# Patch layer of a four-layer stack: half of some B products made on ScalarE from turned operands, partitions ordered state by channel, other C products on GpSimd, and a new plan of slots

## The chip, the cores and the metric

The kernel runs on one core of a Trainium2 chip. A core has five engines with a queue of instructions each: PE (TensorE: matrix products and transposes), DVE (VectorE), ACT (ScalarE: functions from tables, and copies), POOL (GpSimd) and SP (SyncE, which here issues DMAs). Sixteen DMA engines move data between HBM and the on-chip memory SBUF; PE writes into a second on-chip memory, PSUM. The metric is the device time of one execution in microseconds, and the median of 15 runs is given.

## The reference

The input x is (8, 96, 64, 64) in float32. Four layers are added to it in turn, each of the form x = x + layer(gn(x)), where gn is a group normalization: a selective scan over single channels (L0), a gate in the frequency domain (L1), the patch layer (L2) and a deformable 3x3 convolution (L3). Only L2 differs between the two kernels. Cut to what matters:

```python
xz = einsum('bchw,ec->behw', x, in_proj_w)          # 96 -> 2 x 192 channels
xin, z = split(xz, 2); z = silu(z)
t = gelu(batchnorm(conv3x3(xin)))                   # 192 channels
offset = tanh(conv1x1(t)) * 1/(H-1)                 # two offsets for each pixel
x_s = grid_sample_bilinear(xin, grid + offset)
xt = x_s in patches of 4 x 4 pixels                 # L = 16 steps each
xs4 = [xt, xt turned (w,h), and both reversed]      # 4 directions
dts, Bs, Cs = split(einsum(xs4, x_proj_weight))     # 6, 16 and 16 rows
delta = softplus(einsum(dts, dt_projs_weight) + bias)
# for each direction, channel d (192), state n (16), along the 16 steps:
h = h * exp(delta * A[d, n]) + delta * u * B[n]     # "B product" delta*u*B
y[d] = sum_n h * C[n]                               # "C product" h*C
y = sum of the 4 directions + D * u
out = out_proj(layernorm(y) * z)
```

## The kernel before

**Tiling.** L2 is cut into chunks of 512 pixels (8 rows of 64), 8 chunks for each of the 8 images, 64 in all. In a chunk the 512 pixels are 32 patches of 16 steps, and one scan instruction runs over all of them, since delta is set to a huge number at one end of each patch, so that exp gives 0 and the state starts anew (`edges`, L1546). Per chunk and direction there are 192 channels × 16 states = 3,072 rows of 512 steps. They go in groups of 128 partitions × 2 × 512: 32 channels (`GC2`) by 4 state quads (`HS2`) on the partitions, p = d·4 + s, and two of the four states of a quad in the free dimension; `part` 0 and 1 are the two halves of a quad. That makes 12 groups for one direction and 48 for a chunk (`PER` = 48).

**Slots.** `WideSlots.slot` (L442 to L492) issues, slot by slot, what each group needs. In slot t:

- on SP, `dd` for slot t+6 (`AHEAD2`): one DMA that copies delta and delta·u of 32 channels to the 128 partitions, each row four times (L458); both parts share it, so it is issued in every other slot;
- on ACT, for slot t+1, two exps of 128x512 with a scale per partition, from dd into a PSUM tile `ps_d` (L466), of which there are three;
- on DVE, the scan of slot t (L1584, 128x1024), from `ps_d` and `dbu` into `ps_d`;
- on PE, the totals for slot t−2: two groups of matrix products with `k_red2` that sum over the states and add up in `ps_y` (L373);
- on POOL, the B product of slot t+2, delta·u from dd times B from `brep`, into `dbu` in SBUF (L485; 8 buffers);
- on DVE, the C product of slot t−1, `ps_d` times `crep` into `dbu` (L490). For a group named in `LATE2` the scan would write to `dbu` and POOL would make that product; `LATE2` is empty.

DVE's order is thus scan(t), C(t−1), scan(t+1), and so on, and the exp of slot t+1 needs the `ps_d` tile that C(t−2) has read.

`brep` and `crep` are the 16 rows of B or C of one direction, spread over 128 partitions as 4 states × 512 (1 MB, two buffers each). `spread` in `direction` (L1568) issues them on SP; the source is 16 rows in HBM (`bcd`). With the four directions numbered n = 0 to 3, B goes out 2 slots ahead of its pair for odd n and 8 ahead for even n, C one slot behind it or 5 ahead.

**The plan.** Everything else of a chunk is placed by hand in the same slots: `sl.at(slot, engine, function)`, counted from the chunk's first slot B or its pair's first slot T, and run on that engine in the order of `slot`. A chunk's two pairs of directions (`ORDER` = 0, 2, 1, 3) have 24 slots each, and each is slots 0 to 5 first half of the channels of the one direction, 6 to 11 the same half and 12 to 17 the second half of the other, 18 to 23 the second half of the first. `front` (the convolution L1280, gelu L1312, offset L1321, tanh L1341, place L1348, bilinear sampling on POOL L1383, a turned copy of xs L1396, inner L1403, both L1425) runs up to 81 slots ahead of a chunk; `pair` makes delta (products L1483, softplus on ACT and POOL, L1495 to L1538); `gates` makes silu(z); `end` normalizes, gates (L1682), projects, adds x (L1686) and stores (L1719).

ACT holds one table of functions at a time. The default in the loop is the one with exp and ln (`LOG_EXP`); gelu, tanh and silu each load their own and load `LOG_EXP` again (L1313, L1342).

Of the kernel before, what the change touches and what calls it, by code (L numbers as in the profile page):

```python
# [57 lines left out]
def shape_constants():  # L58
# [19 lines left out]
    for d in range(GC2):  # L78
        red[d * HS2 : (d + 1) * HS2, 64 + d] = 1.0
# [33 lines left out]
def lay_out(i):  # L113
# [16 lines left out]
    for k in range(4):  # L130
# [28 lines left out]
        .transpose(2, 3, 0, 1, 4)  # L159
# [84 lines left out]
LOG_EXP = "natural_log_exp_and_others"  # L244
FAR = 1e25
AHEAD = 4
AHEAD2, SPREAD2 = 6, 4
LATE2 = ()
# [193 lines left out]
class WideSlots(Slots):  # L442


    def run(self):
        ts = list(self.plan) + [t + d for t in self.groups for d in (-self.ahead, 3)]
        with self.S.tc.manual_schedule():
            for t in range(min(ts), max(ts) + 1):
                self.slot(t)

    def slot(self, t):
        nc, G = self.S.nc, self.groups.get
        g = G(t + self.ahead)
        if g and g.part:
            g.dd = G(t + self.ahead - 1).dd
        elif g:
            g.dd = new(self.pool, [128, 2, NW], "dd", bufs=self.spread)
            nc.sync.dma_start(  # L458
                g.dd.rearrange("p x l -> p (x l)"),
                g.steps().unsqueeze(1).to_broadcast([self.gc, 128 // self.gc, 2 * NW]),  # L460
            )
        g = G(t + 1)
        if g:
            g.da = new(self.psd, [128, 2, NW], "ps_d")
            for i in range(2):
                nc.scalar.activation(  # L466
                    g.da[:, i, :], g.dd[:, 0, :], AF.Exp, scale=g.a[:, i : i + 1]
                )
        self.side(t, "first")
        g = G(t)  # L470
        if g:
            g.h = g.dbu if g.late else g.da
            g.scan(*(v.rearrange("p i l -> p (i l)") for v in (g.h, g.da, g.dbu)))
# [4 lines left out]
        g = G(t - 3)  # L478
# [4 lines left out]
        if g:  # L483
            g.dbu = new(self.pool, [128, 2, NW], "dbu", bufs=8)
            nc.gpsimd.tensor_tensor(  # L485
                g.dbu, g.dd[:, 1:2, :].to_broadcast([128, 2, NW]), g.b(), ALU.mult
            )
        g = G(t - 1)
        if g:
            (nc.gpsimd if g.late else nc.vector).tensor_tensor(g.dbu, g.h, g.c(), ALU.mult)  # L490
        for engine in ("pool", "dve", "sp", "end"):
# [698 lines left out]
def layer2(S, src, dst, st_in, st_out, images, cp, W, ready, finish):  # L1190
# [3 lines left out]
    with ExitStack() as ctx:  # L1194
# [32 lines left out]
        for k in range(4):  # L1227
# [3 lines left out]
        for k in range(2):  # L1231
            t = new(cp, [CH + 1, 2, NW], f"xs{k}")
# [11 lines left out]
        def front(ch, b, pad, xs, c, B):  # L1244
# [4 lines left out]
            def load():  # L1249
                ch["x"] = new(fp, [CH, 10 * IW], "xl")  # L1250
# [50 lines left out]
            for m, slots, last in (  # L1301
                (0, ((-81, 1), (-80, 2), (-79, 1), (-78, 1), (-77, 1), (-76, 1), (-75, 2)), -74),
                (1, ((-67, 1), (-66, 2), (-65, 1), (-64, 1), (-63, 1), (-62, 1), (-61, 2)), -60),
# [7 lines left out]
            def gelu():  # L1311
                nc.scalar.activation(ch["t"], ch["t"], AF.Gelu)  # L1312
                nc.scalar.preload_act_table_set(LOG_EXP)  # L1313

            sl.at(B - 60, "act", gelu)

            def offset(a):
# [16 lines left out]
                sl.at(B - 59 + a, "pe", pe)  # L1334
                sl.at(B - 58 + a, "first", act)
# [4 lines left out]
            def tanh():  # L1340
                nc.scalar.activation(ch["f"], ch["f"], AF.Tanh)  # L1341
                nc.scalar.preload_act_table_set(LOG_EXP)  # L1342

            def place():
# [3 lines left out]
                nc.scalar.activation(f, f, AF.Identity, bias=sl.half[:CH], scale=0.5)  # L1348

            sl.at(B - 57, "act", tanh)  # L1350
            sl.at(B - 56, "act", place)
# [29 lines left out]
            def sampled():  # L1381
                for k in range(2):
                    nc.gpsimd.tensor_tensor(  # L1383
                        xs[:CH, 0, k * 256 : (k + 1) * 256].rearrange("p (n h w) -> p n h w", h=4, w=4),
# [11 lines left out]
            sl.at(B - 44, "act", lambda: nc.scalar.copy(xs[:CH, 1, :], turned(xs[:CH, 0, :])))  # L1396

            def inner(j):


                def pe():
# [4 lines left out]
                        xs[:CH, 0, :],  # L1406
# [9 lines left out]
                sl.at(B - 23 + j, "pe", pe)  # L1416
                sl.at(B - 22 + j, "first", act)
# [4 lines left out]
            def both():  # L1422
                ch["pa"] = new(psa, [128, NW], "ps_a")
                for o in range(2):
                    nc.tensor.matmul(  # L1425
                        ch["pa"], bc_w[:, o].rearrange("c m s -> c (m s)"), xs[:CH, o, :],
                        start=o == 0, stop=o == 1,
                    )

            def both_out():  # L1430
                ch["bc"] = new(fp, [128, NW], "bc")
# [6 lines left out]
            sl.at(B - 20, "pe", both)  # L1438
            sl.at(B - 19, "first", both_out)
            sl.at(B - 19, "sp", both_store)  # L1440

        def gates(ch, pad, T):
            x = pad[:, 1:9, 1 : IW + 1]

            def gate(m):
# [16 lines left out]
                sl.at(T + m, "pe", pe)  # L1462
                sl.at(T + 1 + m, "first", act)
# [8 lines left out]
            sl.at(T + 2, "act", silu)  # L1472

        def pair(ch, xs, n, T):
# [4 lines left out]
            def first(j):  # L1479
                def pe():  # L1480
# [5 lines left out]
                        xs[:, n, :],  # L1486
# [4 lines left out]
                def act():  # L1491
                    if j == 0:
                        st["e"] = new(fp, [128, BLK, NW], "sp_e")
                        st["m"] = new(fp, [128, BLK, NW], "sp_m")
                    nc.scalar.activation(st["e"][:, j, :], st["p"], AF.Abs)  # L1495
                    nc.scalar.activation(st["m"][:, j, :], st["p"], AF.Relu)  # L1496

                sl.at(T - 26 + j, "pe", pe)
                sl.at(T - 25 + j, "first", act)
# [15 lines left out]
            for m, run in enumerate((exp, one, ln, less)):  # L1515
                sl.at(T - 22 + m, "act", run)

            def block(j):
                e, m, w, s = (lambda k=k: st[k][:, j, :] for k in "emws")

                def add():
                    nc.gpsimd.tensor_tensor(m(), m(), s(), ALU.add)  # L1522
# [4 lines left out]
                def delta():  # L1527
                    if j == 0:
                        pr["d"] = new(fp, [128, BLK, 2, NW], "delta", bufs=2)
                    nc.gpsimd.tensor_tensor(pr["d"][:, j, 0, :], m(), w(), ALU.subtract)  # L1530
# [17 lines left out]
                for i, run in enumerate((add, lost, delta, delta_u)):  # L1548
                    t = BLK * i + j
                    t = T - 18 + t + (t > 4)  # L1550
                    sl.at(t, "pool", run)
                sl.at(t + 1, "act", edges)

            for j in range(BLK):
                first(j)
                block(j)
            return pr

        def direction(ch, pr, xs, k, n, T):
# [4 lines left out]
            def spread(name, what, t):  # L1564
                def run():
# [6 lines left out]
                        .unsqueeze(0)  # L1572
                        .to_broadcast([GC2, HS2, 4 * NW]),
# [665 lines left out]
```

## Time and profile before

| | |
|---|---|
| median of 15 runs | 18,137.27 us (18,088.57 to 18,169.72) |
| profiled execution | 18,137.31 us |
| its span | 18,135.5 us |
| 0 to 3873 us | L0, L1, and the start of L2 |
| 3873 to 14,311 us | L2's 64 chunks |
| 14,311 to 18,135.5 us | end of L2, and L3 |
| busy in the span | DVE 89%, POOL 82%, PE 75%, ACT 55%, PE's weight loads 27% |
| DMA | 2,437 MB in 802,718 packets |

How to read the profile. A group of instructions is one line: source line, engine, operation, output and inputs, number; then busy time in us, the mean of one in ns, and the idle time of the engine ahead of them with what ended most of it. Instructions of an engine overlap a little in the records, so that the mean of one is more than the distance from start to start. The timeline has one line for each instruction: start, length, engine, line, operation. Stretches of time are tabulated by windows: length, busy time of each engine, granted clock (1.00 is full speed), share of the 16 DMA engines that were busy, and what they moved.

### The profile page before, as it was taken

Reading aid. Unit: us, or ns where it says so; the run is one execution under the profiler, and the core shown is the slowest. Engines: PE = TensorE matmul, PEld = TensorE weight load, DVE = VectorE, ACT = ScalarE, POOL = GpSimd, SP = SyncE. Lnnn points to the kernel's source line nnn. Section 1 sums busy time; section 2 is a strip of 40 time slices with the busy share of each in tenths; the row PEclk is TensorE's granted clock in tenths of the full one; section 3 lists DMA queues with packets and bytes.
Section 4 is the critical chain, followed back from the end, with each engine's and each line's share of the span. In section 5 each row is a group of like instructions: output and inputs, shape, how many; then the busy total and the mean of one; then the engine's idle time right before and its main releaser. Section 6 shows DMA issues by size and latency. Waiting matters only on the chain. (4 is left out here: it accounts for less than half of the span.)

```text
span 18135.5 us, 125849 instructions
## 1 busy us (share of the span) xinstructions
PE 13682.9 (75%) x32964; PEld 4891.8 (27%) x32964; DVE 16212.6 (89%) x11111; ACT 10059.6 (55%) x16056; POOL 14788.7 (82%) x8876
## 2 busy tenths in 40 slices
PE   8999998968888888888888888888888644433332
PEld 2322333722222222222222222222222211111111
DVE  7999998679999999999999999999999766767667
ACT  6777775556666666666666666666666311111100
POOL 7999996059999999999999999999999656565555
PEclk8999998989999999999999999999999866666666
DMA  7888886366666665656556666656566445444444
GB/s 125 148 150 148 150 149 117 67 152 138 130 137 132 137 134 134 136 132 139 130 137 132 137 135 133 136 132 139 130 136 132 115 135 153 141 143 136 136 129 121
DMA packets 802718, 2437.25 MB, mean 134 GB/s; under 512 B 259122, under 2 KB 260863, under 8 KB 734829
## 3 DMA queue, kind: packets, MB, share of 16 engines
q1 hardware_dynamic: 654541, 1976.06, 52.3%
q0 software_dynamic: 147456, 453.13, 8.6%
q8 instruction: 262, 4.29, 0.1%
q14 instruction: 459, 3.76, 0.1%
HBM read 1116.39 MB, written 104.46 MB: 67 GB/s over the span
## 5 line engine op out<-in xcount | busy, mean ns | idle before, releaser
L373 PE MATMUL ps_y<-dbu,k_red 128*96 128x512 f32 x15360 | 7597.7, 619 | 1478.4 <-DVE dbu L490 1428.5
L485 POOL TENSOR_TENSOR dbu<-dd,brep 128x1024 f32<-128x1024 f32 x3072 | 7211.7, 2360 | 230.4 <-DMA dd<-delta 114.3
L1584 DVE TENSOR_TENSOR_SCAN ps_d<-ps_d,dbu 128x1024 f32<-128x1024 f32 x3072 | 7014.2, 2283 | 127.0 <-issue 107.1
L466 ACT ACTIVATE ps_d<-dd,l_alog 128x512 f32<-128x512 f32 x6144 | 4242.3, 691 | 3353.2 <-DVE dbu L490 3236.7
L373 PEld LDWEIGHTS ps_y<-dbu,k_red 128*96 128x96 f32 x15360 | 2345.0, 166 | 6387.3 <-DVE dbu L490 3383.7
L490 DVE TENSOR_TENSOR dbu<-ps_d,crep 128x1024 f32<-128x1024 f32 x3072 | 3700.6, 1205 | 0.0
L2073 POOL DMA_INDIRECT v<-t,idx x2304 | 2184.8, 948 | 1565.1 <-DVE s L2100 748.9
L355 POOL TENSOR_TENSOR dbu<-dd,brep 128x1024 f32<-128x1024 f32 x768 | 1793.1, 2355 | 127.9 <-DMA dd<-delta 109.2
L2100 DVE TENSOR_REDUCE s<-v 128x864 f32<-128x3456 f32 x256 | 1554.8, 6073 | 372.7 <-remote 269.9
L2091 DVE TENSOR_TENSOR v<-v,ps_w 128x3456 f32<-128x3456 f32 x256 | 958.4, 3744 | 744.7 <-ACT ps_w L2083 691.8
L735 DVE TENSOR_TENSOR_SCAN ps_d<-ps_d,carry,dbu 128x512 f32<-128x512 f32 x1184 | 1452.7, 1272 | 96.7 <-POOL dbu L355 68.7
L2119 ACT COPY smp<-ps_t 128x768 f32<-128x768 f32 (+1 forms) x512 | 244.5, 529 | 1728.1 <-remote 1040.8
L1280 PE MATMUL ps_a<-pad,woff 96*96 96x512 f32 x2304 | 1146.2, 598 | 26.6 <-ACT pad L1257 24.2
L337 ACT ACTIVATE ps_d<-dd,l_alog 128x512 f32<-128x512 f32 x1536 | 999.5, 682 | 165.4 <-DMA dd<-delta 109.9
L2111 PE MATMUL ps_t<-k_ident,s 128*128 128x128 f32 (+1 forms) x1792 | 326.4, 332 | 985.4 <-issue 622.2
L365 DVE TENSOR_TENSOR dbu<-ps_d,crep 128x512 f32<-128x512 f32 x1344 | 850.4, 673 | 0.0
L1522 POOL TENSOR_TENSOR sp_m<-sp_m,sp_s 128x512 f32<-128x512 f32 x384 | 487.6, 1270 | 369.9 <-ACT sp_s L1510 369.9
L1908 PE MATMUL ps_a<-xpad,l_om 96*27 96x512 f32 x1152 | 593.7, 665 | 32.4 <-issue 30.5
L1925 PE MATMUL ps_u<-k_ident,oc 27*128 27x27 f32 x256 | 32.6, 250 | 751.9 <-ACT oc L1920 687.2
L1280 PEld LDWEIGHTS ps_a<-pad,woff 96*96 96x96 f32 x2304 | 373.6, 164 | 668.0 <-issue 551.8
L2111 PEld LDWEIGHTS ps_t<-k_ident,s 128*128 128x128 f32 (+1 forms) x1792 | 250.3, 169 | 1119.0 <-issue 861.8
L1483 PE MATMUL ps_a<-xs,wd 97*128 97x512 f32 x768 | 428.0, 639 | 139.2 <-ACT sp_m L1496 129.6
(278 smaller groups left out, 15946.9 us busy)
## 6 DMA issues: line engine op xcount, KB each, us to landing
dd<-delta SPq DMA_DIRECT2D x2304, 512.0 KB
brep<-bcd SPq DMA_DIRECT2D x256, 1024.0 KB
crep<-bcd SPq DMA_DIRECT2D x256, 1024.0 KB
v<-t,idx POOLq DMA_INDIRECT x2304
xo<-x SPq DMA_DIRECT2D x128, 192.0 KB
x<-xo SPq DMA_DIRECT2D x128, 192.0 KB
bcd<-bc SPq DMA_DIRECT2D x64, 256.0 KB
xn<-x SPq DMA_DIRECT2D x64, 192.0 KB
```

What stands on the lines that cost most here:

```text
L337: nc.scalar.activation(da, g.dd[:, 0, :], AF.Exp, scale=g.a[:, i : i + 1])
L355: nc.gpsimd.tensor_tensor(g.dbu, g.dd[:, 1:2, :].to_broadcast([128, 2, NW]), g.b(), ALU.mult)
L373: self.S.nc.tensor.matmul(y, self.red[:, HD - self.gc * (g.n + 1) : 2 * HD - self.gc * (g.n + 1)], g.dbu[:, i, :], start=first and i == 0, ...
L466: nc.scalar.activation(g.da[:, i, :], g.dd[:, 0, :], AF.Exp, scale=g.a[:, i : i + 1])
L485: nc.gpsimd.tensor_tensor(g.dbu, g.dd[:, 1:2, :].to_broadcast([128, 2, NW]), g.b(), ALU.mult)
L490: (nc.gpsimd if g.late else nc.vector).tensor_tensor(g.dbu, g.h, g.c(), ALU.mult)
L735: nc.vector.tensor_tensor_scan(out, da, dbu, carry[:, n + i : n + i + 1] if c else 0.0, ALU.mult, ALU.add)
L1280: nc.tensor.matmul(ch["pk"][:HD, :], woff[:, k, m * HD : (m + 1) * HD], pad[:, dy : dy + 8, dx : dx + IW], start=k == 0, stop=k == KT - 1,)
L1584: nc.vector.tensor_tensor_scan(out[:, way], da[:, way], dbu[:, way], 0.0, ALU.mult, ALU.add)
L2073: nc.gpsimd.indirect_dma_start(out=st["v"][:, k].rearrange("p q c -> p (q c)"), out_offset=None, in_=flat, in_offset=bass.IndirectOffsetOn ...
L2091: nc.vector.tensor_tensor(v3, v3, ps_w[:, g % 2, j * 4 * KT : (j + 1) * 4 * KT] .unsqueeze(2) .to_broadcast([128, 4 * KT, CH]), ALU.mult,)
L2100: nc.vector.tensor_reduce(st["s"], st["v"].rearrange("p k q c -> p k c q"), mybir.AxisListType.X, ALU.add,)
```

## The change

It has these parts, all in L2:

1. The partitions of a group are ordered state by channel, p = s·32 + d. `k_red2` and `l2_alog` follow. `dd` now goes out in four DMAs of 32 partitions. The spread of B and C has the same size, and its source is now led by 4 rows with 32 copies of each, where it was led by 32 copies of 4 rows.
2. For every odd n and part 1, 12 of the 48 groups of a chunk, POOL makes only the first half (512) of the B product. The second is made with the steps on the partitions: `rows` transposes delta·u on PE and copies it to SBUF, `over` does that with B, `scaled` multiplies on ACT (32 activations of 128x192 a chunk, with one factor for each partition, a step), and `turn_of` transposes the result back into the group's `ps_d` tile (four transposes a group). The second exp of such a group goes to `dbu`, and its scan is made in two halves.
3. `LATE2` names five groups of each chunk, whose C product POOL makes, two slots behind the scan and not one; their totals come four slots behind it.
4. gelu is followed by a table set that holds exp and tanh, and tanh then loads none; `LOG_EXP` comes back after place. The turned copy of xs is gone, and the matrix products read xs with strides instead. Some buffers are shared or removed (`sp_m`, one of four pads, xl with xo and bc).
5. Nearly all work beside the groups has another slot.

```diff
+EXP_TANH = "exp_and_others"
-LATE2 = ()
+LATE2 = (15, 18, 20, 38, 40)
...
-            nc.sync.dma_start(
-                g.dd.rearrange("p x l -> p (x l)"),
-                g.steps().unsqueeze(1).to_broadcast([self.gc, 128 // self.gc, 2 * NW]),
-            )
+            for p in range(0, 128, self.gc):
+                nc.sync.dma_start(
+                    g.dd[p : p + self.gc].rearrange("p x l -> p (x l)"), g.steps()
+                )
...
             for i in range(2):
+                da = g.dbu if g.turn and i else g.da
+                nc.scalar.activation(da[:, i, :], g.dd[:, 0, :], AF.Exp, scale=g.a[:, i : i + 1])
+            if g.turn:
+                g.turn(g.da[:, 1, :])
...
+            if g.turn:
+                g.scan(g.h[:, 0, :], g.da[:, 0, :], g.dbu[:, 0, :])
+                g.scan(g.h[:, 1, :], g.dbu[:, 1, :], g.da[:, 1, :])
+            else:
+                g.scan(*(v.rearrange("p i l -> p (i l)") for v in (g.h, g.da, g.dbu)))
...
+            n = 1 if g.turn else 2
             nc.gpsimd.tensor_tensor(
-                g.dbu, g.dd[:, 1:2, :].to_broadcast([128, 2, NW]), g.b(), ALU.mult
+                g.dbu[:, :n, :], g.dd[:, 1:2, :].to_broadcast([128, n, NW]), g.b()[:, :n, :],
+                ALU.mult,
             )
+        self.side(t, "pool")
+        g = G(t - 2)
+        if g and g.late:
+            nc.gpsimd.tensor_tensor(g.dbu, g.h, g.c(), ALU.mult)
...
                 nc.scalar.activation(ch["t"], ch["t"], AF.Gelu)
-                nc.scalar.preload_act_table_set(LOG_EXP)
-            sl.at(B - 60, "act", gelu)
+                nc.scalar.preload_act_table_set(EXP_TANH)
+            sl.at(B - 58, "act", gelu)
...
             def tanh():
                 nc.scalar.activation(ch["f"], ch["f"], AF.Tanh)
-                nc.scalar.preload_act_table_set(LOG_EXP)
             def place():
                 nc.scalar.activation(f, f, AF.Identity, bias=sl.half[:CH], scale=0.5)
-            sl.at(B - 57, "act", tanh)
-            sl.at(B - 56, "act", place)
+                nc.scalar.preload_act_table_set(LOG_EXP)
+            sl.at(B - 54, "act", tanh)
+            sl.at(B - 53, "act", place)
...
+            def over():
+                ch["pa"] = new(psa, [128, NW], "ps_a")
+                for k in range(4):
+                    at = slice(k * 128, (k + 1) * 128)
+                    nc.tensor.transpose(ch["pa"][:, at], ch["bc"][:, at], S.ident)
...
-            sl.at(T + 2, "act", silu)
+            sl.at(T + 7, "act", silu)
...
+            def rows(q):
+                def pe():
+                    pr["pa"] = new(psa, [128, NW], "ps_a")
+                    for k in range(2):
+                        at = slice((2 * q + k) * 128, (2 * q + k + 1) * 128)
+                        for j in range(1, BLK):
+                            c = k * 256 + (j - 1) * 128
+                            nc.tensor.transpose(
+                                pr["pa"][:, c : c + 128], pr["d"][:, j, 1, at], S.ident
+                            )
+                def act():
+                    v = pr["pa"].rearrange("p (k c) -> p k c", k=2)
+                    nc.scalar.copy(pr["du"][:, 2 * q : 2 * q + 2, :], v[:, :, 64:])
+            def scaled(m):
+                def run():
+                    k, q = m // HS2, m % HS2
+                    nc.scalar.activation(
+                        pr["prod"][:, k, :, q, :],
+                        pr["du"][:, k, :].rearrange("p (g c) -> p g c", c=GC2),
+                        AF.Copy,
+                        scale=ch["bt"][:, k, n, q : q + 1],
+                    )
...
                         ch["rows"][at : at + NS]
                         .rearrange("(s q) l -> s (q l)", q=4)
-                        .unsqueeze(0)
-                        .to_broadcast([GC2, HS2, 4 * NW]),
+                        .unsqueeze(1)
+                        .to_broadcast([HS2, GC2, 4 * NW]),
...
+            def turn_of(h, g):
+                def run(out):
+                    for k in range(4):
+                        nc.tensor.transpose(
+                            out[:, k * 128 : (k + 1) * 128],
+                            pr["prod"][:, k, 3 * h + g].rearrange("p s c -> p (s c)"),
+                            S.ident,
+                        )
...
+                        turn=turn_of(h, g) if n % 2 and part else None,
...
-                sl.at(B + 76 + h, "pool", lambda h=h: gated(h))
-                sl.at(B + 87 + h, "pe", lambda h=h: out(h))
+                sl.at(B + 62 + h, "pool", lambda h=h: gated(h))
+                sl.at(B + 77 + h, "pe", lambda h=h: out(h))
...
-                (84, "sp", residual), (89, "pe", plus), (90, "first", sum_out),
-                (90, "dve", stats), (91, "sp", store),
+                (74, "sp", residual), (78, "pe", plus), (79, "first", sum_out),
+                (79, "dve", stats), (80, "sp", store),
...
-                gates(ch, pad, B + (42 if b == images[-1] and c == NC - 1 else 61))
+                gates(ch, pad, B + 50)
```

The slots that the diff above leaves out, counted from B or T (before, then after): the convolution −81 to −60, then −74 to −59; offset −59, −56; inner −23, −32; both −20, −37; the products of `pair` T−26, T−29; its exp and ln T−22, T−25; its POOL steps T−18 to T−6, then T−22 to T−11; the two gate products and copies 0 and 1 slots from their start, then 0 and 3. New are `over` at B−35, `rows` at T−10 and T−9, and `scaled` in T−7 to T+5.

## The prediction

> **What bounds the kernel now.** The change touches only the patch layer (L2), so I first cut the profiled execution (18,137.3 us, span 18,135.5; median of the runs 18,137.27) into stages by the busy times in windows: L2's main loop is 3873 to 14311, that is 64 chunks of 163.1 us, each of 48 slots. Columns: length, then busy time of PE, PEld, DVE, ACT, POOL, granted clock, DMA share, GB/s.
>
> ```profile
> 3873.00:14311.00 10438.00, 8771.86 (x18993) 2914.31 (x18993) 10323.73 (x6280) 6989.20 (x10089) 9799.98 (x5314) 0.99 0.60 134
> ```
>
> DVE is 99% busy, POOL 94, PE 84, ACT 67. Next the costliest groups, to see who waits for whom:
>
> ```profile
> L485 POOL TENSOR_TENSOR dbu<-dd,brep 128x1024 f32<-128x1024 f32 x3072 | 7211.7, 2360 | 230.4 <-DMA dd<-delta 114.3
> L1584 DVE TENSOR_TENSOR_SCAN ps_d<-ps_d,dbu 128x1024 f32<-128x1024 f32 x3072 | 7014.2, 2283 | 127.0 <-issue 107.1
> L466 ACT ACTIVATE ps_d<-dd,l_alog 128x512 f32<-128x512 f32 x6144 | 4242.3, 691 | 3353.2 <-DVE dbu L490 3236.7
> ...
> L490 DVE TENSOR_TENSOR dbu<-ps_d,crep 128x1024 f32<-128x1024 f32 x3072 | 3700.6, 1205 | 0.0
> ```
>
> DVE idles 127 us before its scans; ACT idles 3,353 before its exps, nearly all for DVE's C products, which free the PSUM tile. So the loop turns at DVE's pace. DVE's timeline gives that pace (instructions overlap, so I count start to start), and ACT's beside it the one kind of DVE wait:
>
> ```profile
> 9001.89 2.29 DVE L1584 TENSOR_TENSOR_SCAN ps_d<-ps_d,dbu 128x1024 f32<-128x1024 f32 x1
> 9004.09 1.21 DVE L490 TENSOR_TENSOR dbu<-ps_d,crep 128x1024 f32<-128x1024 f32 x1
> ...
> 9057.16 1.21 DVE L490 TENSOR_TENSOR dbu<-ps_d,crep 128x1024 f32<-128x1024 f32 x1
> 9059.06 2.30 DVE L1584 TENSOR_TENSOR_SCAN ps_d<-ps_d,dbu 128x1024 f32<-128x1024 f32 x1 [0.70 <-issue]
> ```
>
> ```profile
> 9053.12 0.76 ACT L1294 ACTIVATE off<-ps_a,sh,sc 96x512 f32<-96x512 f32 x1
> 9053.89 1.28 ACT L1312 ACT_TABLE_LOAD   x1
> 9055.19 1.06 ACT L1312 ACTIVATE off<-off 96x1024 f32<-96x1024 f32 x1
> 9056.26 1.28 ACT L1313 ACT_TABLE_LOAD   x1
> 9057.56 1.42 ACT L466 ACTIVATE ps_d<-dd,l_alog 128x512 f32<-128x512 f32 x2
> ```
>
> A scan takes 2.20 (9001.89 to 9004.09), a C product 1.12 (3.32 from product to product less the scan): 3.32 a slot. 3,072 slots give about 10,190; LayerNorm's scaling and the statistics some 1.7 a chunk, 110; waits 127: 10,430 of 10,438. The wait at 9059.06 is a gelu between two table loads, stacked on another job: the exp starts at 9057.56 and DVE stands 0.70. The 186 "issue" waits (about 3 a chunk) are of this kind.
>
> **The change, part by part.** (1) LATE2: 5 of 48 C products a chunk go from DVE to POOL: 320 × 1.12 = **−358**. This is the gain, provided the others keep up. The moved product stands on POOL two slots after its scan, behind the B product for two slots ahead and the slot's other POOL work; POOL leads the scans by about a slot (scans waited for it 17 us in all of L2), so the scan it needs is done; its totals on PE follow four slots after the scan, inside dbu's 8 buffers.
>
> (2) 768 scans become two scans of 512 steps. L0 has that shape:
>
> ```profile
> 101.32 2.35 DVE L735 TENSOR_TENSOR_SCAN ps_d<-ps_d,dbu 128x512 f32<-128x512 f32 x2 [84.95 <-POOL dbu L355]
> 103.58 1.27 DVE L365 TENSOR_TENSOR dbu<-ps_d,crep 128x512 f32<-128x512 f32 x2
> ```
>
> Two take 2.26 (101.32 to 103.58) against 2.20: 768 × 0.06 = **+46**. Bounds: 0.05 and, by L0's pair with a carry (2.37), 0.17: +38 to +131.
>
> (3) Gelu's return load is now exp's set with tanh; tanh loads nothing, one load a chunk less, and silu, gelu, place and edges get slots of their own. The old waits, **−107**, go. Per slot ACT has 3.32 − 1.35 (exp pair) = 1.97 spare; gelu alone takes 1.28+1.06+1.28 = 3.6, late by 1.7, under a slot's spare. But gelu sits in slot 38 and the late slot lasts only 2.2 on DVE: I allow 0.78 a chunk, **+50**. Other hand-overs 0.4 a chunk, **+25**: nothing to +107 (the old sum).
>
> (4) POOL, per chunk. Before: 48 products at 2.31 (start to start; mean 2.36), 24 softplus steps at 1.23 (3 of them 1.50), front 9.7, gating 2.5: about 153. After: 36 × 2.31 + 12 half products × 1.23 (L0's 512-step row) + 5 C products × 2.31 + the rest = 152. New chunk length 163.1 less the sum below: about 157. POOL fits at 97% and is hidden under DVE; without that cover each us costs 64.
>
> (5) ACT makes the half products: 32 scaled copies 128x192 a chunk, no row. From below the smallest copy, 128x32 at 0.24; from above the exp of 512 with a scale, 0.69; by length 0.39, or 12.5 a chunk, plus copies 4 × 0.48 + 0.24, less the turned copy of xs removed. Fullest new slots: 3 × 0.39 + 0.48 = 1.65, under 1.97; at 0.69, 2.55: 0.6 late, caught up a slot later. I take 0.39: 0, hidden in ACT's 3,353 us of waits (52 a chunk) for DVE. Here the row stands against a rule: the Trainium skill (ScalarE: Activation LUTs, "Rules for kernel authors") has multiplications on VectorE, not ScalarE. DVE's 512-step product (mean 0.67, 0.63 apart) would make 768 × 0.63 = +484 of these.
>
> (6) PE turns the products: 48 transposes for the groups, 16 of delta·u and 4 of bc, 68 a chunk. L3 shows the shape:
>
> ```profile
> 16006.66 0.97 PE L2111 MATMUL ps_t<-k_ident,s 128*96 128x128 f32 x7
> 16007.56 0.43 PE L1925 MATMUL ps_u<-k_ident,oc 27*128 27x27 f32 x4
> ```
>
> 0.13 each: 8.8 a chunk; upper bound, the group's mean with its weight load, .33+.17 = .50: 34. PE was idle 1,666 us in L2, 26 a chunk, of it 1,428 waiting on C products. I take 0.13: 0, hidden there. The wait it adds: a turn waits for its exp, and behind it on PE stand the totals of two slots back, nobody's bottleneck with dbu in 8 buffers; the scan waits for the turn, issued a slot ahead.
>
> (7) Transfers. Partitions become state by channel. dd goes out as 4 DMAs of 32 partitions: 72 more issues a chunk on SP at 0.54 = 39 us, 2.2 for one dd. SP issues in order: a spread or a store that waits would hold the dd issues behind it; x's load and store move to slots 74 and 80, after the sum they wait for, and a dd has six slots, 19.9 us, of lead, of which its window uses 4.9: 0. The b/c spread of 1 MB keeps its size, but its source now leads with 4 rows instead of 32. Two windows of before, a dd alone and a dd with a spread:
>
> ```profile
> 9040.80:9045.70 4.90, 3.90 (x10) 1.18 (x9) 4.90 (x4) 1.95 (x3) 4.90 (x3) 1.00 0.70 107
> 9061.80:9071.20 9.40, 9.40 (x23) 3.58 (x22) 8.89 (x6) 8.55 (x10) 9.40 (x7) 1.00 0.77 167
> ```
>
> dd: 4.90 × .70 × 16 = 55 engine-us; the spread: 9.40 × .77 × 16 − 55 = 61, landing about 9.6 after its issue, under the 19.9 from issue (T−2) to first use (T+4). Lower bound nothing; the upper is rival B. I take 0.
>
> (8) Prologue, tail, shared buffers: **+5**, an estimate: one gating now ends after the last slots, not ahead.
>
> Sum: 18,137 − 358 + 46 − 107 + 50 + 25 + 5 = 17,798: **17,800**. Its own range is 17,700 (stalls gone) to 17,930 (carry-like scans +85, hand-overs as before +57).
>
> **Rivals.** A: POOL decides. Its waits of before that DVE did not cause (230 before L485, 338 on sp_s: 569, 8.9 a chunk) stay: 152 + 8.9 = 160.8 a chunk, −147: 17,990. For: 97% full. Against: the dd waits may go with slack.
>
> B, the slower side: a DMA is dealt out to engines by its outermost count, and a spread that leads with 4 rides on four engines. They carry 8 × 61/4 = 122 a chunk, plus their share of 24 dd, 24 × 55/16 = 82: 204 against 163: +41 × 64 = +2,640: 20,780. It decides once the spreads cost those four over (157 − 82)/8 = 9.4 us, 37 engine-us a spread instead of 61; a price between gives a time between. For: dd was split so that no source leads with 4, the spread was not. Against: no row shows how a DMA is dealt out.
> The Trainium skill (DMA: Bandwidth & Descriptors, "Rules for kernel authors") states it: an outermost size c under 16 confines a DMA to at most c engines. By that rule and the rows the sum is B's 20,780; by the page's 27 GiB/s an engine ("Specifications"), an estimate, a spread takes 9 us on four, 72 a chunk, and the forecast stands. No trace here shows which.
>
> C: PE decides, at .50 a transpose: 137 + 34 = 171 a chunk, +505: 18,640; it tips at (157−137)/68 = 0.30. Against: the seven in 0.90.
>
> D: no change: the gains of (1) and (3) are eaten by new stalls of some 5 a chunk: 18,140.
>
> **How the numbers follow.** Forecast .50, A .14, same .05, B .25, C .06. Faster .64, same (0.2%, ±36 us, what a measurement here tells from nothing) .05, slower .31. The range reaches from 17,700, through A, to 18,600: B's lighter part (.10) is inside; left out are about .03 below and .17 above (the rest of B, half of C).
>
> **What would show it.** After: DVE over 98% of a loop of about 157 a chunk; 2,752 C products on DVE and 320 on POOL; 1,536 scans of 512 steps, pairs 2.26 apart; scaled copies near 0.39; turns 0.13 apart. B shows as POOL waiting on DMA brep or POOL and DVE on crep, with a spread landing 15 us or more after its issue; A as scans waiting for POOL; C as scans waiting for PE. Wrong I would be above all by B.

## The result, and the profile after

The changed kernel takes 20,429.5 us (median of 9 runs, 20,380.5 to 20,492.8), 1.127 times the kernel before (95% interval 1.1256 to 1.1281). The forecast of 17,800 and its range are wrong; rival B's 20,780 is 1.7% off, though not for its reason, as shown below. Runs at a much lower granted clock are left out of all medians here (one of e12's, 33,642 us at a clock of 0.392 where its others show 0.91).

All of the loss is in L2's loop. Its last scan ends at 16,627 us of the changed kernel's profile and at 14,310 us of the one before; the stage ahead of it is the same, and the stage behind it takes 3,842 against 3,826. These are windows of the loop in the changed kernel, with the same columns as before:

```profile
3873.00:16628.00 12755.00, 9947.38 (x23318) 3817.10 (x23318) 10160.99 (x6726) 7555.71 (x12309) 9712.12 (x5633) 0.90 0.43 110
```

A chunk takes 199.3 us where it took 163.1. DVE is busy for 10,161 us, a little less than before, as the late C products should make it, and idles for 2,594, where it idled for 114. The DMA share has fallen from 0.60 to 0.43: the transfers decide, and yet fewer engines are busy. The costliest groups of the changed kernel say what is waited for:

```profile
L492 POOL TENSOR_TENSOR dbu<-dd,brep 128x1024 f32<-128x1024 f32 (+1 forms) x3072 | 6378.9, 2084 | 3001.3 <-DMA dd<-delta 2545.7
...
L1658 DVE TENSOR_TENSOR_SCAN ps_d<-ps_d,dbu 128x1024 f32<-128x1024 f32 (+1 forms) x2752 | 5533.8, 2015 | 1614.4 <-POOL dbu L492 1465.4
L468 ACT ACTIVATE ps_d<-dd,l_alog 128x512 f32<-128x512 f32 x5376 | 3703.4, 689 | 4602.4 <-DMA dd<-delta 2569.7
...
L502 DVE TENSOR_TENSOR dbu<-ps_d,crep 128x1024 f32<-128x1024 f32 x2752 | 3319.9, 1206 | 617.0 <-DMA crep<-bcd 613.3
```

The scans wait for B products, and these for dd; DVE also waits 613 us for `crep` itself. ACT, which used to wait for DVE, waits for dd. So dd, not the spread, is late most of the time. The timeline of SP's queue in the same kernel shows where dd stays (the length is that of the issues as a row, waits between them included):

```profile
10060.87 0.58 SPq L1642 DMA_DIRECT2D brep<-bcd  x1
10061.55 2.43 SPq L460 DMA_DIRECT2D dd<-delta  x4
10064.07 0.58 SPq L1642 DMA_DIRECT2D crep<-bcd  x1
10064.76 44.32 SPq L460 DMA_DIRECT2D dd<-delta  x24
```

Two spreads go out 3.2 us apart, and the next 24 pieces of dd, six dds, take 44 us to be issued where 24 × 0.58 would be 14. And this is the DMA view of the 40 us from 10,060, one digit for each microsecond, the busy share of the 16 engines in tenths:

```profile
DMA  3858959322132222222499722222222115898892
GB/s 80 214 94 205 234 139 205 78 57 90 41 98 57 90 82 82 98 98 94 127 242 250 164 74 90 98 98 106 98 102 98 66 57 139 205 205 205 205 213 62
```

Two long rows of 2: about a quarter of 16 engines, four, and some 57 to 106 GB/s. Counted in the trace's DMA packets, between 4,000 and 14,000 us:

```
packets of 8 KB (spread)            before   changed
mean of one, us                      0.425     0.453
time with exactly 4 in flight, us       95     4,674
time with more than 5 in flight, us  2,006        10
one spread alone, first to last, us    5.2      15.9
two that overlap, us                  13.5      31.3
```

The last two rows are medians; in the changed kernel only six spreads stand alone there, and 70 pairs overlap. Mostly four packets are in flight, and hardly ever more than five, where it was up to 16: a spread is carried by four engines, and stays in flight three times as long. That is the first half of rival B's mechanism. The second, that the work of the four fills the chunk, is taken up with the runs.

### The profile page after: what moved, and what is told of

It reads as the page before. It is cut to its first block, busy times and chain, and to the rows that moved or that the text cites. A ratio compares the mean times of both kernels' runs of the same rounds, so it can differ in the third digit from the quotient of the medians.

```text
span 20469.0 us, 145606 instructions
## 1 busy us (share of the span) xinstructions
PE 14868.0 (73%) x37316; PEld 5801.6 (28%) x37316; DVE 16051.1 (78%) x11559; ACT 10635.2 (52%) x18296; POOL 14701.8 (72%) x9195
## 4 chain that ended last, share of the span: by engine, by line
DMA 38%; PE 22%; DVE 12%; issue 9%; another core or an unknown queue 7%; ACT 7%; POOL 4%; SPq 1%; DVEq 0%; POOLq 0%; ACTq 0%
DMA crep<-bcd 12%; DMA brep<-bcd 11%; DMA dd<-delta 10%; PE ps_y L374 8%; DMA xl<-x 4%; DVE ps_d L1658 4%; DVE dbu L502 3%; PE ps_a L1292 2%; PE ps_a L1995 2%; POOL dbu L492 2%; PE ps_k L649 2%; DVE ps_d L747 1%; ACT ps_d L468 1%; SPq L460 1%
## 5 line engine op out<-in xcount | busy, mean ns | idle before, releaser
L492 POOL TENSOR_TENSOR dbu<-dd,brep 128x1024 f32<-128x1024 f32 (+1 forms) x3072 | 6378.9, 2084 | 3001.3 <-DMA dd<-delta 2545.7
L1658 DVE TENSOR_TENSOR_SCAN ps_d<-ps_d,dbu 128x1024 f32<-128x1024 f32 (+1 forms) x2752 | 5533.8, 2015 | 1614.4 <-POOL dbu L492 1465.4
L468 ACT ACTIVATE ps_d<-dd,l_alog 128x512 f32<-128x512 f32 x5376 | 3703.4, 689 | 4602.4 <-DMA dd<-delta 2569.7
L356 POOL TENSOR_TENSOR dbu<-dd,brep 128x1024 f32<-128x1024 f32 x768 | 1793.0, 2354 | 128.5 <-DMA dd<-delta 101.9
L1685 PE MATMUL ps_d<-k_ident,prod 128*128 128x128 f32 x3072 | 566.2, 315 | 751.6 <-ACT ps_d L468 751.6
L338 ACT ACTIVATE ps_d<-dd,l_alog 128x512 f32<-128x512 f32 x1536 | 999.5, 682 | 146.1 <-DMA dd<-delta 92.2
L1658 DVE TENSOR_TENSOR_SCAN ps_d<-dbu,ps_d 128x512 f32<-128x512 f32 x704 | 864.9, 1228 | 74.4 <-DVE ps_d L1658 1.8
L1611 ACT ACTIVATE prod<-turned,bt 128x192 f32<-128x192 f32 x2048 | 825.5, 446 | 0.0
L1685 PEld LDWEIGHTS ps_d<-k_ident,prod 128*128 128x128 f32 x3072 | 422.7, 161 | 1244.3 <-ACT ps_d L468 1059.3
L1658 DVE TENSOR_TENSOR_SCAN dbu<-ps_d,dbu 128x1024 f32<-128x1024 f32 (+1 forms) x320 | 659.9, 2062 | 135.3 <-ACT ps_d L468 135.3
L499 POOL TENSOR_TENSOR dbu<-dbu,crep 128x1024 f32<-128x1024 f32 x320 | 754.4, 2357 | 2.8 <-DVE dbu L1658 2.8
```

The lines of the kernel that those rows point to most:

```text
L338: nc.scalar.activation(da, g.dd[:, 0, :], AF.Exp, scale=g.a[:, i : i + 1])
L356: nc.gpsimd.tensor_tensor(g.dbu, g.dd[:, 1:2, :].to_broadcast([128, 2, NW]), g.b(), ALU.mult)
L468: nc.scalar.activation(da[:, i, :], g.dd[:, 0, :], AF.Exp, scale=g.a[:, i : i + 1])
L492: nc.gpsimd.tensor_tensor(g.dbu[:, :n, :], g.dd[:, 1:2, :].to_broadcast([128, n, NW]), g.b()[:, :n, :], ALU.mult,)
L1658: nc.vector.tensor_tensor_scan(out[:, way], da[:, way], dbu[:, way], 0.0, ALU.mult, ALU.add)
L1685: nc.tensor.transpose(out[:, k * 128 : (k + 1) * 128], pr["prod"][:, k, 3 * h + g].rearrange("p s c -> p (s c)"), S.ident,)
```

## The experiments

Each run stands against the kernel before, run beside it on the same chip. On the chip of the first four that took 18,139 us; on those of the others 17,310 and 17,305. The L2 loop is as long there (from the first scan to the last, 10,454 us in e11 and 10,453 in e1); it is the stage behind it (L3) that is shorter, 3,003 us against 3,806 in the same two profiles. So each run is compared by its difference from its own before; the changed kernel itself is 2,292 us over its own.

| run | what | ratio to before (95%) | us over before |
|---|---|---|---|
| e1 | changed, spread in four DMAs | 1.0012 (1.0001 to 1.0023) | +16 |
| e2 | before, with part 1 alone | 1.1585 (1.1562 to 1.1608) | +2,873 |
| e3 | e2, spread in four DMAs | 0.9999 (0.9988 to 1.0009) | −3 |
| e4 | changed, only B's spread in four | 1.0532 (1.0509 to 1.0554) | +956 |
| e5 | e1, C product between half scans | 0.9972 (0.9961 to 0.9983) | −54 |
| e6 | changed, dd 8 slots ahead | 1.1271 (1.1254 to 1.1288) | +2,201 |
| e7 | e1, LATE2 empty | 1.0081 (1.0065 to 1.0096) | +137 |
| e8 | e1, states of turned groups in SBUF | 1.0884 (1.0869 to 1.0899) | +1,524 |
| e9 | e5, slot 42 late, not 38 | 0.9993 (0.9984 to 1.0002) | −13 |
| e10 | changed, dd in eight DMAs | 1.3106 (1.3086 to 1.3126) | +5,383 |
| e11 | e1, dd in eight DMAs | 1.0010 (1.0001 to 1.0020) | +19 |
| e12 | e5, without part 2 | 1.0059 (1.0043 to 1.0074) | +105 |

### Is it the spread's leading count? (e1, e2, e3)

e1 changes one thing in the changed kernel: four DMAs of 32 partitions, whose sources lead with 32 copies.

```diff
-                    nc.sync.dma_start(dr[name]..., ch["rows"][at : at + NS]
-                        .rearrange("(s q) l -> s (q l)", q=4)
-                        .unsqueeze(1).to_broadcast([HS2, GC2, 4 * NW]))
+                    for s in range(HS2):
+                        nc.sync.dma_start(
+                            dr[name][s * GC2 : (s + 1) * GC2].rearrange("p q l -> p (q l)"),
+                            ch["rows"][at + 4 * s : at + 4 * s + 4]
+                            .rearrange("(o q) l -> o (q l)", q=4).to_broadcast([GC2, 4 * NW]),
+                        )
```

> The changed kernel, but the spread of B and C goes out as four DMAs of 32 partitions, each with a source that leads with 32 copies. Theory (a spread whose source leads with 4 rows is carried by four DMA engines, and nothing else is wrong): the forecast of before comes true, 17,800 (17,700 to 17,930). Rival 1 (the turned products, the C products on POOL or the new slots cost it): no gain, above 19,500. Rival 2 (too many DMA issues on SP, dd in four pieces each): 12 more issues for each pair make it worse, above 20,430.

18,155 us. The spread's form alone is worth 2,276 of the 2,292 us lost. In the DMA packets one spread takes 5.2 us again, and POOL's wait before its B products falls from 3,001 us to 21. But the gain isn't there either: e1 is no faster than before, so the theory in its second half ("and nothing else is wrong") fell too. That is taken up below.

e2 is the other side: the kernel before with the new order of partitions, dd in four pieces and the spread led by 4 rows, and nothing else of the change. e3 is e2 with e1's edit.

```diff
-        red[d * HS2 : (d + 1) * HS2, 64 + d] = 1.0
+        red[d::GC2, 64 + d] = 1.0
...
-        .transpose(2, 3, 0, 1, 4)
+        .transpose(3, 2, 0, 1, 4)
...
-            nc.sync.dma_start(g.dd.rearrange("p x l -> p (x l)"),
-                g.steps().unsqueeze(1).to_broadcast([self.gc, 128 // self.gc, 2 * NW]))
+            for p in range(0, 128, self.gc):
+                nc.sync.dma_start(g.dd[p : p + self.gc].rearrange("p x l -> p (x l)"), g.steps())
...
-                        .unsqueeze(0).to_broadcast([GC2, HS2, 4 * NW]),
+                        .unsqueeze(1).to_broadcast([HS2, GC2, 4 * NW]),
```

> The kernel before with part 1 alone: state by channel, dd in four DMAs, the spread's source led by 4 rows. Theory: nearly the whole loss is here, about 20,400 (20,100 to 20,700). Rival 1: 18,140. Rival 2: also about 20,400.

> As the layout alone, but with the spread in four DMAs of 32 partitions. Theory: as before the change, 18,140 within 40. Rival 2 (issues on SP): above 20,000. Rival 1: 18,140.

e2 takes 21,011 us, 600 more than expected and more than the whole changed kernel; e3 takes 18,135, just as before. So part 1 costs 2,870 us as written and nothing with the spread on all engines, and four times as many dd issues cost nothing by themselves.

### By which way does a slow spread cost? (e4, e6, e10, e11)

I had priced it as work on four engines. e4 takes B's half of the spreads off them, to all 16:

```diff
+                    if name == "c":
+                        nc.sync.dma_start(...)      # one DMA, led by 4 rows
+                        return
                     for s in range(HS2):
```

> The changed kernel with B's spread split in four DMAs and C's still led by 4 rows. The four engines then carry, by the packets of the changed kernel's trace (0.45 us for 8 KB, 0.27 for 4 KB), 4 x 32 x 0.45 + 24 x 8 x 0.27 = 110 us a chunk, under 157. If the four engines' throughput decides, as rival B was priced: 17,800. If it is the lateness of each single spread and what SP holds back behind it: half of the loss stays, about 19,100. Rival 1: above 19,500.

19,095 us: 956 of the 2,292 us stay. By the expectation's sum the four engines then have 110 us of work in a chunk; it leaves out their share of B's spread, 4 × 8 × 0.45, and with it the sum is some 124 us, still under 157. Work alone doesn't explain it. The other candidates were dd queued behind the spread on those four engines, and SP. The program's DMAs use eight semaphores in turn, so that each DMA on SP first waits for the one issued eight before it. Seven DMAs can follow a spread in flight, and the eighth stands; with dd in four pieces that is less than two dds, four slots. e6 issues dd two slots earlier, with a fifth buffer of dd and, to make room, one of `dbu` less.

```diff
-AHEAD2, SPREAD2 = 6, 4
+AHEAD2, SPREAD2 = 8, 5
...
-            g.dbu = new(self.pool, [128, 2, NW], "dbu", bufs=8)
+            g.dbu = new(self.pool, [128, 2, NW], "dbu", bufs=7)
...
```

> The changed kernel, spread still led by 4 rows, with dd issued 8 slots ahead and not 6 (five buffers of dd, and seven of dbu to make room). If dd is late because it queues on the four engines behind a spread of 14.5 us, longer than the 13.3 us from its issue to the B product two slots ahead: two slots more recover most of the loss, under 19,300. If SP holds it back (each DMA waits for the one eight issues earlier, so that a spread in flight lets at most seven after it out): 20,430 within 200. If the four engines are full: the same, 20,430.

2,201 us over before, 91 less than without the edit. POOL's wait for dd falls from 2,546 to 824 us, but it now waits 981 us for `brep`, DVE's wait for `crep` rises from 613 to 1,013, and again 24 pieces of dd behind a pair of spreads take 45 us to issue. POOL also waits 417 us for PE, where it was 47; the buffer of `dbu` that is gone may add to that. Two slots of lead alone are not what is missing. Work on four engines and SP were both still open. e10 changes the number of issues and not the bytes, and e11 is its control:

```diff
-            for p in range(0, 128, self.gc):
+            for p in range(0, 128, 16):
                 nc.sync.dma_start(
-                    g.dd[p : p + self.gc].rearrange("p x l -> p (x l)"), g.steps()
+                    g.dd[p : p + 16].rearrange("p x l -> p (x l)"),
+                    g.steps()[p % self.gc : p % self.gc + 16],
                 )
```

> The changed kernel, spread led by 4 rows, with each dd in eight DMAs of 16 partitions: the same bytes and rows on the same engines, twice the issues. If the loss comes by SP (a DMA waits for the one eight issues before, so that no more than one dd passes a spread in flight, two slots): much worse, above 1.20 of before. If the four engines' work alone decides: 1.127 within 0.01 as without the edit.

> The same eight pieces of dd with the spread in four DMAs on all engines, as a control: if the issues themselves cost nothing, 1.001 of before.

With fast spreads eight pieces are free (e11 is 3 us from e1); with slow ones they cost 3,091 us more than four (5,383 less 2,292). SP's timeline in e10:

```profile
10016.62 0.58 SPq L1643 DMA_DIRECT2D brep<-bcd  x1
10017.30 20.36 SPq L460 DMA_DIRECT2D dd<-delta  x8
10037.77 0.58 SPq L1643 DMA_DIRECT2D crep<-bcd  x1
10038.44 19.27 SPq L460 DMA_DIRECT2D dd<-delta  x8
```

Behind each spread eight issues, one dd, take 20 us: the eighth stands until the spread has landed. The same can be read from SP's waits in the loop of the changed kernel; these are the two longest (us in total, number, longest):

```profile
SPq L460 <- DMA crep<-bcd: 2768.9, 256, 15.5
SPq L460 <- DMA brep<-bcd: 2702.7, 255, 15.6
```

SP stands 5,472 us of 12,755 for a spread, 10.7 for each. In e10 it is 7,434 us, in e4 3,749, in e6 5,484, as without that edit, and in e1 120. POOL's wait for dd goes along in e10 and e4: 5,299 us and 769, against 2,546.

The four engines, on the other hand, are not full. With 8 × 32 packets of 8 KB and 24 × 8 of 4 KB each, at the mean times of each trace, they have 168 us of work in the changed kernel's chunk of 199.3, and 202 in e10's of 246.9. That is an estimate, since the trace doesn't name a packet's engine. It also shows that e10 alone doesn't part the two: its packets take longer (0.524 and 0.356 us, against 0.453 and 0.271 in the changed kernel), so the work grew with the issues. So a slow spread costs in good part what stands behind it on SP. How the changed kernel's 2,276 us divide between this and the four engines' work isn't settled; an order of partitions that allows dd in a single DMA was not tried.

### Where did the forecast's gain go? (e5, e7, e8, e9, e12)

With the spread mended, e1's loop is 10,453 us from the first scan to the last, against 10,437 before: its 16 us are there. These are DVE's longest waits in that loop:

```profile
DVE dbu L1658 <- ACT ps_d L468: 98.7, 62, 1.6
DVE ps_d L1658 <- POOL bl_bot L1388: 74.6, 47, 1.9
DVE ps_d L1658 <- POOL delta L1551: 59.3, 62, 2.4
DVE ps_d L1658 <- PE ps_d L1685: 57.8, 56, 1.2
```

In us, number and the longest. And this is DVE's timeline in e1 over a turned group between whole ones:

```profile
9058.22 1.21 DVE L502 TENSOR_TENSOR dbu<-ps_d,crep 128x1024 f32<-128x1024 f32 x1
9059.34 1.22 DVE L1658 TENSOR_TENSOR_SCAN ps_d<-ps_d,dbu 128x512 f32<-128x512 f32 x1
9060.66 1.23 DVE L1658 TENSOR_TENSOR_SCAN ps_d<-dbu,ps_d 128x512 f32<-128x512 f32 x1
9061.80 1.21 DVE L502 TENSOR_TENSOR dbu<-ps_d,crep 128x1024 f32<-128x1024 f32 x1
```

The halves are 1.32 apart, the second is 1.14 from the product: 2.46 for the pair, not 2.26. In the program the second half waits on a semaphore for the first, which writes to the same `ps_d` tile. (The 64 pairs that write to a `dbu` tile are 1.13 apart all the same; why these differ is open.) e5 puts the C product of the group before between them:

```diff
                 g.scan(g.h[:, 0, :], g.da[:, 0, :], g.dbu[:, 0, :])
+                p = G(t - 1)
+                if p and not p.late:
+                    nc.vector.tensor_tensor(p.dbu, p.h, p.c(), ALU.mult)
                 g.scan(g.h[:, 1, :], g.dbu[:, 1, :], g.da[:, 1, :])
...
-        if g and not g.late:
+        n = G(t)
+        if g and not g.late and not (n and n.turn):
             nc.vector.tensor_tensor(g.dbu, g.h, g.c(), ALU.mult)
```

> The changed kernel with the spread in four DMAs; in a turned group DVE makes the C product of the group before between the two half scans, not after them. The trace has the halves 1.32 us apart where two independent scans of 512 are 1.13 apart. If the second half waits for the first one's result: about 9 of 12 groups a chunk lose the wait, 9 x 64 x 0.19 = 110 less, 18,045. If the operands' places (PSUM second, SBUF first) make it slow: 18,155 as without the edit.

0.9972, the only run that is faster than both kernels, by 0.3%. In its timeline the wait is gone:

```profile
9005.37 1.21 DVE L506 TENSOR_TENSOR dbu<-ps_d,crep 128x1024 f32<-128x1024 f32 x1
9006.49 1.22 DVE L1662 TENSOR_TENSOR_SCAN ps_d<-ps_d,dbu 128x512 f32<-128x512 f32 x1
9007.62 1.21 DVE L479 TENSOR_TENSOR dbu<-ps_d,crep 128x1024 f32<-128x1024 f32 x1
9008.74 1.22 DVE L1662 TENSOR_TENSOR_SCAN ps_d<-dbu,ps_d 128x512 f32<-128x512 f32 x1
```

From scan to product 1.13, on to the second half 1.12: the operands' places cost nothing, the wait did. Against e1 it gains 71 us where I expected 110; DVE's wait for ACT ahead of late scans grew from 92 to 132 beside it (4,000 to 13,400 us).

e8 takes the wait away in another way, with h of the turned groups in dbu:

```diff
-            g.h = g.dbu if g.late else g.da
+            g.h = g.dbu if g.late or g.turn else g.da
```

> The changed kernel with the spread in four DMAs; a turned group's scans write into dbu in SBUF, as those of the late groups do, which the trace shows 1.12 apart. If C products from SBUF cost what those from PSUM do (1.12): 0.22 x 704 = 155 less, 18,000. If the two sources in SBUF slow DVE or POOL: above 18,155.

1.088: the scans are 1.13 apart, as expected, but the C product now has both sources in SBUF. The 704 of these take 3.64 on average, the 2,048 from PSUM still 1.20. This is one of them, DVE and POOL in time order:

```profile
9340.00 14.92 DVE L502 TENSOR_TENSOR dbu<-dbu,crep 128x1024 f32<-128x1024 f32 x1
9340.11 1.29 POOL L1557 TENSOR_TENSOR delta<-delta,sp_w 128x512 f32<-128x512 f32 x1
...
9352.29 1.54 POOL L1563 TENSOR_TENSOR delta<-delta,u 128x512 f32<-128x512 f32 x1
9354.84 1.21 DVE L1764 TENSOR_TENSOR yc<-yc,ps_a 96x1024 f32<-96x1024 f32 x1
```

POOL works without a gap from 9340.1 to 9353.8; the product ends 1.1 us later, about its own length. The Trainium skill (SBUF — State Buffer, "Who interferes with whom") says that a DVE instruction with two SBUF inputs contends with a GpSimd instruction that reads SBUF; the trace agrees, and shows DVE kept out for nine POOL instructions in a row. My upper side of e8 had named it, without a price.

e7 asks what part 3 is worth.

```diff
-LATE2 = (15, 18, 20, 38, 40)
+LATE2 = ()
```

> The changed kernel with the spread in four DMAs and LATE2 empty: DVE makes all C products. By the sum: 320 x 1.12 = 358 more, less the waits that the late slots bring by the trace (ACT 99, POOL up to 134): 18,280 to 18,410. If the late products gain nothing, since POOL is the bound: 18,155 or less.

1.0081, 121 us above e1, just under what was expected: of 358 us saved on DVE two thirds come back as waits. In e7 DVE's scans wait 57 us in all in the loop, in e1 305 (one of 19 at its start left out).

e12 asks the same of part 2: no transposes, no scaled copies, all B products whole on POOL, on top of e5.

```diff
-                        turn=turn_of(h, g) if n % 2 and part else None,
+                        turn=None,
...
-            sl.at(B - 35, "pe", over)
-            sl.at(B - 34, "first", over_out)
...
-            rows(0)
-            rows(1)
...
-                    sl.at(T + t, "act", scaled(m))
```

> The kernel with the spread in four DMAs, without part 2: POOL makes all B products whole, no transposes, no scaled copies, whole scans; the five C products stay on POOL. POOL then has 152 + 12 x 1.08 = 165 us a chunk. If POOL's sum decides: 1.007 of before or more. If POOL's work by the sum isn't what decides: DVE loses the split scans and the waits for PE, 0.989.

1.0059, 159 us above e5 and near the 1.007 of POOL's sum; this rests on the time alone. So part 2 without part 3 (e7) and part 3 without part 2 (e12) are both slower than the kernel before, and the two together gain 0.3% with e5's order. Parts 1, 4 and 5 without either were not run.

e9 was meant to take away the wait for ACT. In e5 the gelu of slot 38 stands like this:

```profile
9032.69 0.72 ACT L468 ACTIVATE dbu<-dd,l_alog 128x512 f32<-128x512 f32 x1
9033.44 1.28 ACT L1328 ACT_TABLE_LOAD   x1
9034.73 1.06 ACT L1328 ACTIVATE off<-off 96x1024 f32<-96x1024 f32 x1
9035.80 1.28 ACT L1329 ACT_TABLE_LOAD   x1
9037.10 1.42 ACT L468 ACTIVATE ps_d<-dd,l_alog 128x512 f32<-128x512 f32 x2
```

The next exps start 3.69 after the end of the last pair's second, and the scan of slot 40 stands 2.28 at 9038.62. e9 lets slot 42 be late in the place of 38.

```diff
-LATE2 = (15, 18, 20, 38, 40)
+LATE2 = (15, 18, 20, 40, 42)
```

> The kernel with the spread in four DMAs and the C product between the half scans, with LATE2 = (15, 18, 20, 40, 42): slot 38, in which ACT has gelu and its table, keeps its C product on DVE. The trace shows DVE waiting 2.27 us a chunk for ACT at the scan of slot 40. If the slot shortened beside gelu makes it: 1.1 to 2.3 less a chunk, 0.989 to 0.993 of before. If gelu alone makes it, or POOL comes late with the new place: 0.997 as without the edit, or more.

0.9993, 41 us worse than e5. In the same stretch the late scans' wait for ACT falls from 132 to 77 us and the wait for the sampling on POOL from 78 to 16, but waits for which the profile names no releaser rise from 35 to 175; POOL's wait for the late scans grows from 96 to 203. It missed: the new place is as bad as the one it replaced, and why is open.

## Why the prediction was wrong, point by point

**The step that failed is (7)**: "Lower bound nothing; the upper is rival B. I take 0." The row of before had a 1 MB spread in 9.6 us on engines that all took part; nothing in it carried over to a source led by 4 rows. Two bounds that far apart, decided by one unmeasured rule on how a DMA is dealt out, deserved more than the .25 that B had. e1 and e3 show that the whole loss is this term.

**Rival B's size came out by luck, and its tipping point was wrong.** 204 us a chunk was forecast, 199.3 came. But the size came from work on four engines that fills the chunk, and by the packets they have about 168 us of it; in e4 some 124 us, under 157, still cost 5.3%. What (7) missed is the queue. A DMA that lasts holds back the one eight issues behind it on SP, and all after that (5,472 us in the loop), which four pieces to a dd had made a short way. (7) saw that a spread that waits would hold dd; it didn't see that one in flight does, and counted SP's issue time, 2.2 us, but not these waits. It also gave dd "six slots, 19.9 us, of lead", where POOL's product is made two slots ahead and four slots, 13.3 us, were left, less than the 15.9 of a spread; but two slots more (e6) recovered almost nothing.

**The rule and the rate beside rival B.** The rule of the Trainium skill (DMA: Bandwidth & Descriptors, "Rules for kernel authors"), at most c engines for an outermost size c, is what the packets show: four in flight. Its 27 GiB/s an engine ("Specifications"), by which the forecast would have stood, is not reached: 8 KB in 0.453 us, the mean, is 18 GB/s, with dd on the same engines; half of the packets took 0.349 us or less, 23 GB/s.

**(1), late C products: size right on DVE, net wrong.** 320 products are gone from DVE and stand on POOL at 2.36 each. Net of waits they gained 121 of 358 us (e7).

**(2), half scans: +46 forecast, about +185 measured in e1** (0.26 for 704 pairs; the 64 late pairs have no wait). Its upper bound, 131, was too low: the row was L0's pair on two separate `ps_d` tiles, and here both halves are in one, with a wait of 0.19 between them. e5 shows the wait.

**(3), ACT and hand-overs: 75 forecast, 305 measured in e1's loop.** ACT took 99 for the gelu beside shortened slots, where I allowed 50. The rest is what I called hand-overs, 25: POOL's bursts 134, PE's turns 58. Rival A had the right engine but not the right form: POOL's sum of 152 us a chunk was right (9,700/64 = 151.6 in e1) and does not fill the chunk, but in the slots with bilinear sampling and softplus it falls behind for a while. So −358 + 185 + 305 − 127 of the old waits = +5 where e1's loop has +16.

**(4), (5), (6) held.** Scaled copies are 0.35 apart (0.39 forecast), the four transposes of a turn take 0.50 (0.13 each), and PE and ACT were not the bound; rival C is out.

## What to carry to other kernels

When a change turns the order of partitions, read anew what each DMA's source leads with: a size that is the same in bytes can go from all engines to four. Price a slow DMA by what its queue holds back behind it and by the real distance from issue to first use, not only by the work of the engines that carry it. And work that is moved off a full engine comes back as waits wherever the slots it goes to are already full for a moment; an average over the chunk doesn't show that.

## What the runs showed of the hardware that was not expected

- A 1 MB DMA whose source is led by 4 rows has four packets in flight and takes 15.9 us; the same bytes led by 32 copies take 5.2 us.
- With DMAs that wait for the one eight issues before, one such DMA held the queue for 10.7 us on average (5,472 us for 511 of them in the changed kernel's loop).
- A DVE product with both sources in SBUF took up to 17.8 us, and 3.64 on average (half of them 1.27 or less) against 1.20 from PSUM, while POOL worked on SBUF without a gap (e8).
- A DVE half scan that waits for the one just before it, in the same `ps_d` tile, starts 0.19 us later than one that doesn't (1.32 against 1.13), and an independent product put between the two hides it (e5).
